# The chosen tokens' keys made token-major in four column tiles, and the shared latent copied by DMA

## The chip, the cores and the metric

One NeuronCore of a Trainium2 chip runs the whole program. The metric is the device time of one execution in microseconds (us). Five engines work side by side and meet at semaphores: TensorE (PE, matmul; PEld is its weight load), VectorE (DVE), ScalarE (ACT), GpSimd (POOL) and SyncE (SP, which here only issues DMAs).

## The reference, cut to what matters

The reference is a two-layer network on `x` of shape (8, 512, 128): a WKV layer and a quantised linear layer, then an attention layer of three branches and a recurrent layer. The change touches the attention layer alone. Of that, for one batch element:

```python
nq  = _rms(x @ w_cq, g_qnorm)                     # 512 x 96
q   = concat([nope(nq @ w_dq_nope), rope(nq @ w_dq_rope)])   # 16 heads, 32 + 64
ckv = _rms(x @ w_ckv, g_kvnorm)                   # 512 x 32, the shared latent
k1  = concat([ckv @ w_dk_nope, rope(x @ w_krope) / 16])
idx = sort(top_k(x @ w_imp, 32)); sel = x[idx]    # the 32 chosen tokens
ks  = sel @ w_selk                                # 32 x 16 heads x (32 + 64)
ks  = concat([ks[..., :32], rope(ks[..., 32:])])
vs  = sel @ w_selv
kw, vw = x @ w_wink, x @ w_winv
a1 = attn(q, k1, v1, causal); a2 = attn(q, ks, vs); a3 = attn(q, kw, vw, causal)
out = gate0 * a1 + gate1 * a2 + gate2 * a3
```

All data are float32.

## The kernel before

The main loop walks over "units". A unit is one batch element `b` (8 of them), one group `g` of four heads (4 groups), one causal branch `a` (0 for `a1`, 1 for `a3`) and one set of 128-row query blocks (three sets: block 3, blocks 0 and 1, block 2): 8 x 4 x 2 x 3 = 192 units. Round `i` of the loop makes the scores of unit `i + 2` (`score`, L777), lowers them by mask and row maximum on VectorE (`lowered`, L789), exponentiates on ScalarE (`raised`, L798), scales the rows on GpSimd (`normalised`, L807), transposes the probabilities of unit `i` on TensorE (`weigh`, L821), copies them out on ScalarE (L599), and after every third unit multiplies with the values (`values`, L835). Feeds between them (`group_inputs`) make the next group's queries, keys and values: `qR` and `k3R` by `rotary` (L630), `qN`, `qA` and `k3N` by `plain` (L606, copied out at L608), the values at L661.

The order of instructions on PE, DVE, ACT and POOL is the order in which the Python code issues them (`manual_schedule`), and each engine runs its own list in that order. The rest of the work runs as generators ("chains") beside the units: `layer0` (WKV, L315 to L388, and the quantised linear layer, L399 to L425, with `mx_quantize`, L140 to L170), `before` (which is `prepare(b)`: normalisation, latents, shared keys, gate, top-k, chosen keys), and `recurrence`. Four times in a round `advance` lets each chain take one step, if the number that it yielded has been counted down. A chain that yields `M` goes on only at the fourth place of a round; one that yields 0 goes on at the next place. `need(name, b)` advances all chains until something is ready, and in it `M` steps run at once.

Of `prepare(b)` two parts concern the change.

`shared_keys(b)`, run some rounds ahead of the batch element's first scores: `k1R` is the rotated shared key (two matmuls L630, `turn` on VectorE L615 to L622 and on GpSimd L621 and L623). Then `k1N`, the shared latent in four copies below one another, 128 rows: a matmul (`k1l`, L708) of the latent, rows 96 to 127 of `nqT`, with `rep`, four 32x32 identities side by side, and a copy out on ScalarE with a scale per row (`g4`, L709). Between its three parts it yields `M`, so each has a round to itself. The scores of branch 0 read `k1N` against `qA`.

`chosen_keys(b)`: `sel` (128 features x 32 tokens, written by ScalarE at L535) is the moving operand; each of 12 matmuls has a 128x128 block of weights as its stationary operand and gives 32 columns. Eight (L680, `sk`) make the two halves of the rotary part, each half in a PSUM tile of its own, turned from PSUM on VectorE (L615, L616, L620, L622) and finished on GpSimd (L621, L623) as `sR`; four (L689, `sNp`) make the other part, copied out by ScalarE (`sN`, L690). Each of these three is followed by a yield of `M`. Then `sV` (a matmul at L694, eight VectorE instructions of 32 rows at L698). `sR` and `sN` are stationary operands of the chosen branch's scores (`chosen`, L739), which go through PSUM into 32x32 block transposes on VectorE (L745), a softmax (L748 to L756) and the product with `sV` (L722). `attend_chosen(b, 0)` calls `need("chosen", b)`.

A float32 matmul stands in the trace as two records, so 12 matmuls are 24 of PE. In shapes such as `32*128` the first number is the rows of the stationary block and the second its columns.

PSUM: the pool `ps_t` has three buffers, shared by all that `bank` hands out; the scores have four single buffers (`ps_s`), the output one (`ps_o`). The queue of SP carries the loads of `x`, and writes `x1all` and `h2all` of each batch element to DRAM for the tail, in the order of the program.

Of the kernel before, what the change touches and what calls it, by code (L numbers as in the profile page):

```python
# [11 lines left out]
FP = mybir.dt.float32  # L12
U32 = mybir.dt.uint32
AF = mybir.ActivationFunctionType
# [9 lines left out]
HG = 4  # L24
# [34 lines left out]
def adaln_kernel(ctx: ExitStack, tc: tile.TileContext, x, pa, pb, pc, pt, out):  # L59
# [10 lines left out]
    mask = const.tile([128, T], FP, name="mask")  # L70
    wmix = {n: [const.tile([128, 128], FP, name=f"{n}{i}") for i in range(2)] for n in ("wkT", "wvT", "wrT")}
    wn, u, nu = (const.tile([128, 1], FP, name=n) for n in ("wn", "u", "nu"))
    rep = const.tile([128, 128], FP, name="rep")
    wqT = const.tile([128, 128], FP, name="wqT")
    gbias = const.tile([128, B], FP, name="gbias")
    sil0 = const.tile([128, B], FP, name="sil0")
# [96 lines left out]
    with tc.tile_pool(name="start", bufs=1) as p1, tc.tile_pool(name="startps", bufs=2, space=PSUM) as pp:  # L173
        wa = p1.tile([128, _width(A_COLS)], FP, name="wa")
        wa2 = p1.tile([128, _width(A2_COLS)], FP, name="wa2")
        WA = _views(wa, A_COLS) | _views(wa2, A2_COLS)

        load(0)
        nc.sync.dma_start(out=wa, in_=pa[:, 0 : _width(A_COLS)])
        load(1)  # L180
        nc.sync.dma_start(out=wa2, in_=pa[:, _width(A_COLS) :])
        for t, p in ((wb, pb), (wt, pt), (wc, pc)):
            nc.sync.dma_start(out=t, in_=p)
        make_identity(nc, ident)


        for l in range(2):
            c_in = WA[f"cT{l}"]

            sg = p1.tile([128, B], FP, name=f"sg{l}")  # L190
            S.activation(sg, c_in, AF.Tanh, scale=0.5)
            si = sil0 if l == 0 else p1.tile([128, B], FP, name="sil1")
            V.tensor_scalar(sg, sg, 0.5, 0.5, ALU.mult, ALU.add)
            V.tensor_tensor(si, sg, c_in, ALU.mult)
            ps = pp.tile([128, 6, B], FP, name=f"modps{l}", tag="modps")
            for j in range(6):
                PE.matmul(ps[:, j, :], lhsT=WA[f"wmod{l}"][:, j * 128 : (j + 1) * 128], rhs=si, start=True, stop=True)
            m = mods[l]
            V.tensor_copy(m, ps)
            for j in (1, 4):  # L200
                V.tensor_scalar(m[:, j, :], m[:, j, :], 1.0, None, ALU.add)
            for j in (2, 5):
                sgn = p1.tile([128, B], FP, name=f"sgn{l}{j}")
                V.tensor_scalar(sgn, m[:, j, :], 0.0, 2.0, ALU.is_ge, ALU.mult)
                mag = p1.tile([128, B], FP, name=f"mag{l}{j}")
                V.scalar_tensor_tensor(mag, m[:, j, :], -1.0, m[:, j, :], ALU.mult, ALU.max)
                V.tensor_scalar(mag, mag, 0.25, None, ALU.max)
                V.scalar_tensor_tensor(m[:, j, :], sgn, -1.0, mag, ALU.add, ALU.mult)


        for n, m in (("wkT", "tmk"), ("wvT", "tmv"), ("wrT", "tmr")):
            om = p1.tile([128, 1], FP, name=f"om_{m}")
            V.tensor_scalar(om, WA[m], -1.0, 1.0, ALU.mult, ALU.add)
            V.tensor_scalar(wmix[n][0], WA[n], WA[m], None, ALU.mult)
            V.tensor_scalar(wmix[n][1], WA[n], om, None, ALU.mult)
        S.activation(wn, WA["w"], AF.Exp)
        V.tensor_scalar(wn, wn, -1.0, None, ALU.mult)
        V.tensor_copy(u, WA["u"])
        V.tensor_scalar(nu, WA["u"], -1.0, None, ALU.mult)


        wq = p1.tile([128, 4, 32], FP, name="wq")
        for _ in mx_quantize(
            wq, WA["fw"].rearrange("p (n k) -> p n k", k=32), 4,
            lambda n: p1.tile([128, 4, 32], FP, name=f"q{n}_w"), "w",
        ):
            pass
        wps = pp.tile([128, 128], FP, name="wps", tag="modps")
        PE.transpose(wps, wq.rearrange("p n k -> p (n k)"), ident)
        S.copy(wqT, wps)  # L230
        V.tensor_scalar(gbias, mod0[:, 5, :], WA["fbias"], None, ALU.mult)

        ps = pp.tile([QL, H * KVL], FP, name="foldp", tag="foldp")
        for g in range(NG):
            PE.matmul(
                ps[:, g * 128 : (g + 1) * 128], lhsT=WA["wdqT"][:, g * QL : (g + 1) * QL],
                rhs=WA["wdkT"][:, g * 128 : (g + 1) * 128], start=True, stop=True,
            )  # L240
        wd = WB["wd"]
        qscale = 1.0 / math.sqrt(HD)
        gq = p1.tile([QL, 1], FP, name="gq")
        V.tensor_scalar(gq, WB["g"][0:QL, :], qscale, None, ALU.mult)
        S.activation(wabs, ps, AF.Copy, scale=gq)
        V.tensor_scalar(wd[0:QL, :], wd[0:QL, :], gq, None, ALU.mult)
        V.tensor_scalar(wd[QL:128, 0:512], wd[QL:128, 0:512], WB["g"][QL:128, :], None, ALU.mult)
        V.tensor_scalar(WB["wkr"], WB["wkr"], 1.0 / H, None, ALU.mult)

        for j in range(HG):  # L250
            V.tensor_copy(rep[QL:128, j * KVL : (j + 1) * KVL], ident[QL:128, QL:128])

        for n in ("ufT", "uiT", "ucT", "uoT", "bf", "bi"):
            V.tensor_scalar(WC[n], WC[n], 0.5, None, ALU.mult)

        G.memset(mask, 0.0)
        G.affine_select(
            mask, mask, pattern=[[-1, T]], compare_op=ALU.is_ge, fill=NEG, base=T - 128, channel_multiplier=1
        )
# [33 lines left out]
    def bank(shape, name):  # L293
        return ps_t.tile(shape, FP, name=name, tag="t")
# [305 lines left out]
        else:  # L600
            V.tensor_copy(dst, src)

    def plain(pool, name, b, g, src, w):

        ps = bank([128, T], f"{name}p_{b}_{g}")
        PE.matmul(ps, lhsT=w[:, g * 128 : (g + 1) * 128], rhs=src, start=True, stop=True)  # L606
        dst = pool.tile([128, T], FP, name=f"{name}_{b}_{g}", tag=name)
        S.copy(dst, ps)  # L608
        return dst

    def turn(i, dst, ps, tabs, pool, tags, key):
# [13 lines left out]
    def rotary(pool, name, key, src, w, temps):  # L625

        dst = pool.tile([128, 2, T], FP, name=f"{name}_{key}", tag=name)
        for i in range(2):
            ps = bank([128, T], f"{name}m{i}_{key}")
            PE.matmul(ps, lhsT=w[:, i * 128 : (i + 1) * 128], rhs=src, start=True, stop=True)  # L630
            turn(i, (dst[:, 0, :], dst[:, 1, :]), ps, (cosT, sinT), *temps, f"{name}_{key}")
            if i == 1:
                rot_of[name] = dst
            yield

    def group_inputs(b, g):
# [5 lines left out]
        yield from rotary(pq, "qR", f"{b}_{g}", nq, wq_r[:, hs], (p1, ("rt0", "rt1")))  # L642
        qN = plain(pq, "qN", b, g, nq, wq_n)
        yield
        qA = plain(pq, "qA", b, g, nq, wabs)
        q_of[b, g] = rot_of["qR"], qN, qA
        yield
        yield from rotary(p1, "k3R", f"{b}_{g}", hT, ww_r[:, hs], (p1, ("rt0", "rt1")))
# [21 lines left out]
    def chosen_keys(b):  # L670

        _, _, gate, sel = made_of[b]
        shape = [128, NG, KEEP]
        tabs = [tab[:, 0:KEEP].unsqueeze(1).to_broadcast(shape) for tab in (cosT, sinT)]
        sR = pb_.tile([128, 2, NG, KEEP], FP, name=f"sR_{b}", tag="sR")
        for i in range(2):
            yield M
            ps = bank(shape, f"sk{i}_{b}")
            for g in range(NG):
                PE.matmul(  # L680
                    ps[:, g, :], lhsT=ws_r[:, (2 * g + i) * 128 : (2 * g + i + 1) * 128], rhs=sel[:, 0, :],
                    start=True, stop=True,
                )
            turn(i, (sR[:, 0], sR[:, 1]), ps, tabs, pw, ("p2", "p3"), f"sk_{b}")
        yield M
        sN = pb_.tile([128, NG, KEEP], FP, name=f"sN_{b}", tag="sN")
        ps = bank([128, NG, KEEP], f"sNp_{b}")
        for g in range(NG):
            PE.matmul(ps[:, g, :], lhsT=ws_n[:, g * 128 : (g + 1) * 128], rhs=sel[:, 0, :], start=True, stop=True)  # L689
        S.copy(sN, ps)  # L690
        yield M
        sV = pb_.tile([128, 2, NG, VD], FP, name=f"sV_{b}", tag="sV")
        ps = bank([128, NG, HG, VD], f"sv_{b}")
        PE.matmul(ps, lhsT=sel, rhs=WB["wselv"], start=True, stop=True)  # L694
        for h in range(2):
            for j in range(HG):
                at = home(j, h)
                V.tensor_scalar(sV[at, h], ps[at, :, j, :], gate[at, 1:2], None, ALU.mult)  # L698
        chosen_of[b] = (sR[:, 0], sR[:, 1], sN), sV

    def shared_keys(b):

        hT, nqT, _, _ = made_of[b]
        for _ in rotary(pb_, "k1R", f"{b}", hT, WB["wkr"], (pw, ("p2", "p3"))):
            yield M
        k1N = pb_.tile([128, T], FP, name=f"k1N_{b}", tag="k1N")
        ps = bank([128, T], f"k1l_{b}")
        PE.matmul(ps, lhsT=rep[QL:128, :], rhs=nqT[QL:128, :], start=True, stop=True)  # L708
        S.activation(k1N, ps, AF.Copy, scale=WB["g4"])  # L709
        k1_of[b] = rot_of["k1R"], k1N  # L710

    def home(j, h):
# [401 lines left out]
```

## Time and profile before

| | before |
|---|---|
| median of 3 runs | 1780.53 us (1780.38 to 1781.57) |
| profiled execution | 1776.72 us |
| its span | 1774.9 us |
| TensorE clock granted, mean | 0.963 |
| PE, DVE, ACT, POOL busy | 93%, 71%, 66%, 52% |
| DMA queue of SP, share of 16 engines | 2.9% |

A busy share is an average, and matmuls are pipelined, so PE at 93% is not PE at its peak. The chain of waits is followed back from the last instruction: at each step it goes to what released that instruction, or to the one before it on its engine. A microsecond taken from a piece of the chain can shorten the run; one taken from work off the chain cannot, until it is on it. The first 95 us are the start (loads, layer 0 of the first elements); the units run from there to about 1740 us.

### The profile page before, as it was taken

What the parts mean: (1) busy time and instruction counts of PE and PEld (TensorE: products, weight loads), DVE (VectorE), ACT (ScalarE), POOL (GpSimd) and SP (SyncE); (2) the same over time, 40 slices, a digit from 0 to 9 for tenths busy, and PEclk for the clock granted to TensorE, in tenths of its full rate; (3) what the DMA queues carried; (4) which work ended last, traced back from release to release, by engine and by line L of the source; (5) the groups of instructions that cost most, each with busy time, mean ns of one, the idle gap of its engine ahead of it and who ended that gap; (6) DMA issues with size and microseconds to landing.
All of it is one profiled execution on the core that took longest, in us unless ns stands there. A gap on an engine that the chain in (4) does not pass through costs nothing.

```text
span 1774.9 us, 40101 instructions
## 1 busy us (share of the span) xinstructions
PE 1651.0 (93%) x14865; PEld 964.7 (54%) x14865; DVE 1253.5 (71%) x4246; ACT 1166.3 (66%) x3262; POOL 914.6 (52%) x1370
## 2 busy tenths in 40 slices
PE   4388999899999999999999999999999999999997
PEld 2245555555555555555555555555556555655663
DVE  6678777875876698776886777776885766665542
ACT  1244777566765777667776677677666777767782
POOL 1145556544754475644755455545656455545651
PEclk8698999899999999999999999999999999999998
DMA  4000000000000000000000000000000000000012
GB/s 168 1 1 1 2 1 1 7 2 13 2 1 7 13 2 1 2 13 7 1 2 1 13 1 2 1 14 7 1 1 1 13 8 1 2 13 8 13 37 66
DMA packets 13395, 20.24 MB, mean 11 GB/s; under 512 B 784, under 2 KB 8976, under 8 KB 13072
## 3 DMA queue, kind: packets, MB, share of 16 engines
q1 hardware_dynamic: 13200, 17.67, 2.9%
q8 instruction: 119, 1.95, 0.4%
q14 instruction: 76, 0.62, 0.1%
HBM read 11.90 MB, written 5.77 MB: 10 GB/s over the span
## 4 chain that ended last, share of the span: by engine, by line
PE 71%; DVE 20%; POOL 3%; ACT 3%; issue 2%; DMA 1%; SPq 0%; POOLq 0%; ACTq 0%; DVEq 0%
PE s L777 23%; PE t L821 13%; PE o L835 7%; DVE p L789 6%; PE qRm L630 2%; PE s L739 2%; PE k3Rm L630 2%; PE v1p L661 2%; PE v0p L661 2%; PE op L846 2%; PE o L722 1%; PE qAp L606 1%; PE k3Np L606 1%; POOL p L807 1%; PE qNp L606 1%
## 5 line engine op out<-in xcount | busy, mean ns | idle before, releaser
L807 POOL TENSOR_SCALAR p<-p,rs 128x512 f32<-128x512 f32 (+3 forms) x1024 | 556.2, 564 | 503.6 <-DVE rs L803 318.6
L789 DVE CUSTOM_DVE_ANT_0 p<-s,mask 128x512 f32<-128x512 f32 (+3 forms) x1024 | 443.0, 478 | 223.4 <-PE s L777 221.5
L798 ACT ACTIVATE p<-p,nm 128x512 f32<-128x512 f32 (+3 forms) x1024 | 560.9, 553 | 15.3 <-DVE nm L789 15.3
L599 ACT COPY pT<-t 128x384 f32<-128x384 f32 (+1 forms) x768 | 355.4, 522 | 200.2 <-PE t L821 198.6
L821 PE MATMUL t<-ident,p 128*128 128x128 f32 x2560 | 361.9, 279 | 18.5 <-DVE k3R L616 5.8
L821 PEld LDWEIGHTS t<-ident,p 128*128 128x128 f32 x2560 | 273.8, 141 | 141.6 <-issue 106.0
L777 PE MATMUL s<-k3R,qR 32*128 32x512 f32 (+3 forms) x2048 | 197.7, 471 | 6.4 <-DVE nm L789 5.3
L777 PE MATMUL s<-k1R,qR 32*128 32x512 f32 (+3 forms) x2048 | 192.0, 458 | 10.0 <-DVE nm L789 7.8
L798 ACT ACTIVATION_READ_ACCUMULATOR p<-p,nm 128x1 f32 x1024 | 195.8, 191 | 0.0
L835 PE MATMUL o<-pT,v 128*32 128x512 f32 (+3 forms) x2048 | 151.1, 436 | 0.0
L777 PEld LDWEIGHTS s<-k3R,qR 32*128 32x128 f32 x2048 | 100.4, 192 | 91.5 <-DVE nm L789 31.2
L777 PEld LDWEIGHTS s<-k1R,qR 32*128 32x128 f32 x2048 | 98.6, 188 | 93.6 <-issue 34.7
L835 PEld LDWEIGHTS o<-pT,v 128*32 128x32 f32 x2048 | 60.0, 109 | 109.4 <-issue 98.4
L777 PE MATMUL s<-k1N,qA 32*128 32x512 f32 (+3 forms) x1024 | 98.3, 430 | 0.0
L777 PE MATMUL s<-k3N,qN 32*128 32x512 f32 (+3 forms) x1024 | 98.2, 437 | 0.0
L789 DVE DVE_READ_ACCUMULATOR2_ANT nm<- 128x1 f32 x1024 | 83.2, 81 | 0.0
L599 ACT COPY accT<-o 128x512 f32<-128x512 f32 x32 | 18.8, 588 | 89.4 <-PE o L835 89.4
L749 POOL TENSOR_TENSOR p<-p,m 128x512 f32<-128x512 f32 x32 | 33.6, 1049 | 83.6 <-DVE m L748 83.5
L621 POOL TENSOR_TENSOR k3R<-k3R,rt_k3R 128x512 f32<-128x512 f32 x32 | 40.8, 1273 | 66.1 <-DVE rt_k3R L620 66.1
L630 PE MATMUL qRm<-nqT,wb 96*128 96x512 f32 x128 | 68.9, 621 | 2.0 <-ACT pT L599 1.0
L777 PEld LDWEIGHTS s<-k3N,qN 32*128 32x128 f32 x1024 | 56.3, 192 | 24.6 <-issue 17.3
L777 PEld LDWEIGHTS s<-k1N,qA 32*128 32x128 f32 x1024 | 55.6, 188 | 22.7 <-issue 10.1
(314 smaller groups left out, 2492.6 us busy)
## 6 DMA issues: line engine op xcount, KB each, us to landing
wb<-pb_dram SPq DMA_DIRECT2D x1, 3475.0 KB, 14.7
x<-x_dram SPq DMA_DIRECT2D x8, 256.0 KB, 3.8
x1all<-x SPq DMA_DIRECT2D x7, 256.0 KB, 2.3
h2all<-h SPq DMA_DIRECT2D x7, 256.0 KB, 2.0
h2o<-h2all SPq DMA_DIRECT2D x7, 256.0 KB, 2.6
x_first<-x1all SPq DMA_DIRECT2D x4, 256.0 KB, 4.2
out_dram<-x_first SPq DMA_DIRECT2D x4, 256.0 KB, 2.5
out_dram<-x SPq DMA_DIRECT2D x4, 256.0 KB, 2.4
```

Of the source, the lines that this page charges most:

```text
L599: S.copy(dst, src)
L606: PE.matmul(ps, lhsT=w[:, g * 128 : (g + 1) * 128], rhs=src, start=True, stop=True)
L621: G.tensor_tensor(lo, lo, r[0], ALU.subtract)
L630: PE.matmul(ps, lhsT=w[:, i * 128 : (i + 1) * 128], rhs=src, start=True, stop=True)
L661: PE.matmul(ps[:, c, :], lhsT=hT[:, cs] if i else nqT[QL:128, cs], rhs=(WB["wwinv"] if i else wv_1)[:, g * 128 : (g + 1) * 128], start=Tru ...
L739: PE.matmul(sp[h][to, :], lhsT=k[js, g, :], rhs=q[js, h * half : (h + 1) * half], start=(i == 0), stop=(i == 2), skip_group_check=True,)
L777: PE.matmul(un.s[j][:, at : at + n], lhsT=q[js, n - 128 : n], rhs=k[js, 0:n], start=(i == 0 and at == 0), stop=(i == 2), skip_group_check= ...
L789: V.tensor_tensor_reduce(out=un.p[:, j, at : at + n], in0=un.s[j][:, at : at + n], in1=mask[:, T - n :], scale=-1.0, scalar=3.4e38, op0=AL ...
L798: S.activation(p, p, AF.Exp, bias=un.nm[:, j, i : i + 1], scale=-1.0, accum_out=un.rs[:, j, i : i + 1])
L807: G.tensor_scalar(p, p, un.rs[:, j, i : i + 1], 1.0, ALU.mult, ALU.mult)
L821: PE.transpose(tp[:, k, :], un.p[:, j, at : at + 128], ident)
L835: PE.matmul(out_ps[js, c * 128 :], lhsT=v[:, c, js], rhs=pT[:, j, at[0] : at[-1] + 1 : step, :], start=not a and c == 0, stop=False, skip_ ...
```

## The change

`chosen_keys` swaps the operands: `sel` (128x32) is the stationary operand and the weights are streamed. Heads 0 to 3 of a group go to four column tiles of 32 columns, so that four matmuls write four groups of 32 PSUM partitions: four of 256 columns for the rotary part, four of 128 for the other, all in one PSUM tile, tokens in partitions. Two VectorE transposes by 32x32 blocks (128x256 into `kT`, 128x128 into `sN`) give the layout that was there before. `turn` then reads `kT` in SBUF where it read PSUM. The copy of `sN` on ScalarE is gone. The yields change: matmuls and transposes come at once, each `turn` follows at the next place of a round, and only then comes an `M`.

`shared_keys` issues four DMAs on SP's queue that copy the latent to the four row groups of `k1N`, before the rotary part; the matmul L708, the scaled copy L709 and the constant `rep` (four VectorE copies at the start) are gone, and two of three yields of `M` with them. The scale `g4` moves to the copy of `qA`: `plain` uses `activation` with AF.Copy and a scale, which is 1.0 for `qN` and `k3N` and `g4` for `qA`.

```diff
-        for j in range(HG):
-            V.tensor_copy(rep[QL:128, j * KVL : (j + 1) * KVL], ident[QL:128, QL:128])
...
-    def plain(pool, name, b, g, src, w):
+    def plain(pool, name, b, g, src, w, scale=1.0):
...
-        S.copy(dst, ps)
+        S.activation(dst, ps, AF.Copy, scale=scale)
...
-        qA = plain(pq, "qA", b, g, nq, wabs)
+        qA = plain(pq, "qA", b, g, nq, wabs, WB["g4"])
...
+        ps = bank([128, 3 * NG, 32], f"sk_{b}")
+        heads = [(w.rearrange("k (n j d) -> k j n d", j=HG, d=32), at, n) for w, at, n in ((ws_r, 0, 2 * NG), (ws_n, 2 * NG, NG))]
+        for w, at, n in heads:
+            for j in range(HG):
+                PE.matmul(
+                    ps[32 * j : 32 * (j + 1), at : at + n, :], lhsT=sel[:, 0, :], rhs=w[:, j], start=(at == 0), stop=True,
+                    skip_group_check=True,
+                )
+        kT = work("p2", [128, NG, 2, KEEP], f"kT_{b}")
+        V.transpose(kT.rearrange("p g i k -> p (g i k)"), ps[:, 0 : 2 * NG, :].rearrange("p n d -> p (n d)"))
+        sN = pb_.tile(shape, FP, name=f"sN_{b}", tag="sN")
+        V.transpose(sN.rearrange("p g k -> p (g k)"), ps[:, 2 * NG :, :].rearrange("p n d -> p (n d)"))
         sR = pb_.tile([128, 2, NG, KEEP], FP, name=f"sR_{b}", tag="sR")
+        yield 0
         for i in range(2):
-            yield M
-            ps = bank(shape, f"sk{i}_{b}")
-            for g in range(NG):
-                PE.matmul(
-                    ps[:, g, :], lhsT=ws_r[:, (2 * g + i) * 128 : (2 * g + i + 1) * 128], rhs=sel[:, 0, :],
-                    start=True, stop=True,
-                )
-            turn(i, (sR[:, 0], sR[:, 1]), ps, tabs, pw, ("p2", "p3"), f"sk_{b}")
-        yield M
-        sN = pb_.tile([128, NG, KEEP], FP, name=f"sN_{b}", tag="sN")
-        ps = bank([128, NG, KEEP], f"sNp_{b}")
-        for g in range(NG):
-            PE.matmul(ps[:, g, :], lhsT=ws_n[:, g * 128 : (g + 1) * 128], rhs=sel[:, 0, :], start=True, stop=True)
-        S.copy(sN, ps)
-        yield M
+            turn(i, (sR[:, 0], sR[:, 1]), kT[:, :, i, :], tabs, pw, ("p3", "p3") if i == 0 else ("p3", "p1"), f"sk_{b}")
+            yield 0 if i == 0 else M
...
     def shared_keys(b):
-        for _ in rotary(pb_, "k1R", f"{b}", hT, WB["wkr"], (pw, ("p2", "p3"))):
-            yield M
         k1N = pb_.tile([128, T], FP, name=f"k1N_{b}", tag="k1N")
-        ps = bank([128, T], f"k1l_{b}")
-        PE.matmul(ps, lhsT=rep[QL:128, :], rhs=nqT[QL:128, :], start=True, stop=True)
-        S.activation(k1N, ps, AF.Copy, scale=WB["g4"])
+        for j in range(HG):
+            nc.sync.dma_start(out=k1N[j * KVL : (j + 1) * KVL, :], in_=nqT[QL:128, :])
+        for i, _ in enumerate(rotary(pb_, "k1R", f"{b}", hT, WB["wkr"], (pw, ("p2", "p3")))):
+            if i == 0:
+                yield M
```

More of the change, by code (lines that the diff above doesn't have):

```diff
@@ L72, in adaln_kernel @@
     wn, u, nu = (const.tile([128, 1], FP, name=n) for n in ("wn", "u", "nu"))
-    rep = const.tile([128, 128], FP, name="rep")
     wqT = const.tile([128, 128], FP, name="wqT")
```

## The prediction, made before the changed kernel ran

> **What bounds the kernel now.** I read the page first, the chain of waits above all.
>
> ```profile
> PE 1651.0 (93%) x14865; PEld 964.7 (54%) x14865; DVE 1253.5 (71%) x4246; ACT 1166.3 (66%) x3262; POOL 914.6 (52%) x1370
> ...
> PE 71%; DVE 20%; POOL 3%; ACT 3%; issue 2%; DMA 1%; SPq 0%; POOLq 0%; ACTq 0%; DVEq 0%
> ```
>
> The chain is PE for seven tenths and DVE for two. Summed in eight stretches from 95 to 1720 us, PE has about 1190 of 1625 us, or 73%. So PE work taken away in the middle of the run is worth about 0.73 of itself, and ACT work (3%) next to nothing. Next I asked the chain, in order of time, for the pieces that the change removes. Around the start of batch element 4 (counted from 0) they stand in it one after the other:
>
> ```profile
> 936.77 0.85 PE sk L680 x8
> ...
> 944.59 0.85 PE sk L680 x8
> 945.44 1.80 PE k3Rm L630 x4
> 947.24 0.56 PE o L722 x8
> ...
> 952.53 0.81 PE sNp L689 x8
> 953.35 0.94 PE k3Np L606 x2
> ```
>
> The columns are start, length, what. The three groups of 8 records cost 2.51 us of chain here, and PE waits for nothing between 928 and 962 us. The same groups stand in the chain at elements 5, 6 and 7, two of the three at element 3; `k1l` stands there at 285.79, 473.59, 666.36, 865.10, 1074.54, 1285.42 and 1482.08 us, 1.05 us each time. The first three elements look different. For element 0 the chain has
>
> ```profile
> 144.27 3.62 PE sk L680 x16
> 147.90 1.72 PE sNp L689 x8
> 149.62 0.02 issue
> 149.64 0.28 ACT sN L690
> 149.92 0.04 issue
> 149.96 2.07 PE sv L694 x2
> 152.03 2.56 PE s L739 x48
> ```
>
> that is PE at half clock (the windows from 144 to 152 us show 0.50 granted), and for element 1
>
> ```profile
> 348.40 1.66 POOL q L160
> 350.06 0.07 issue
> 350.13 1.60 POOL q L164
> 351.73 0.02 issue
> 351.75 0.69 DVE q L168
> 352.45 0.20 DVE sR L615
> ```
>
> Here the chosen keys' turn stands on DVE behind the quantiser's `q`, which waits for POOL; PE is idle 4.29 us until `sR` is there (354.23). Element 2 repeats it (3.72 us idle, until 542.42).
>
> **The change, part by part.** The changed program's order of instructions, laid beside the old one, gives positions and no times.
>
> *The chosen keys on PE.* Removed: 24 records, 2.5 us at full clock (0.85 + 0.85 + 0.81). Added: 16 records in four column tiles. No row has this shape (128 rows, 32 columns, 256 or 128 streamed). The nearest is `o` L722: 8 records of 256 columns in four tiles, 0.56 us. I take 0.56 for the rotary part and half, 0.28, for the other: 0.84. From below: `o` L835, 32 records of 512+384+256+128 columns in four tiles, 2.29 us in the chain, by columns 384/1280 x 2.29 = 0.69. From above: tiles that do not overlap, each load (L835's mean 109 ns) behind the other, 16 x 0.109 = 1.74. Gain 1.67 per element (0.8 to 1.8); for elements 3 to 7: 8.4 us.
>
> L722's 0.56 lies above what its columns need: `op` L846 takes 3.45 us for 8 records of 512, so 0.43 each, and two records of 256 in a row are 0.43; 0.13 us is for getting in and out. The Trainium skill (TensorEngine Tiling (Array Packing), Key Properties) says that changing the tiling mode drains TensorE, which speaks against the change, since the old groups had the 128x128 shape of their neighbours; if each group paid two drains of 0.13 beyond the row, the sum would be 8 x 0.26 = 2.1 us less. The same page's Performance Considerations advise just this swap for 32 streamed columns.
>
> *Element 0.* 16 records at half clock 1.7 us, so done at 145.95; two transposes on DVE 0.65, three short steps (`rsqrt`, 0.16 to 0.20 each) 0.6, turn 0.4, three more 0.6, turn 0.4: 148.6; POOL two of 0.46, the first starting the chosen scores: about 149.2 against 152.03. Gain 2.8.
>
> *Elements 1 and 2.* In the new order the transposes and turns stand before the quantiser's first `q` on DVE, and POOL's work for `sR` between its two long ones. Element 1: `z` ends at 344.35, transposes 0.65, rotary 1.2, `e` 1.04, turn 0.4, `m` 1.78: 349.4; POOL's first `q` 1.66, `sR` 0.47: PE goes on at 351.6 against 354.23. Element 2: 535.26 + 0.65 + 0.44 + 0.4 + 0.78 = 537.5, + 1.65 + 0.47 and issue = 539.8 against 542.42. Gain 2.6 each. But the `q` steps passed over are only put behind the chosen scores, where DVE has still to do them, ahead of row maxima that PE waits for. I take half of these and of element 0: (2.8 + 5.2) x 0.5 = 4.0, bounds 0 and 8; the clock that the wait pulls down (`s` L739 2.81 us at 354 against 1.46 at 956) could give 2 x 1.35 more.
>
> *The shared latent.* Removed from PE: 1.05 us at elements 1 to 7, 7.35; nothing at element 0, where the first scores wait for POOL's `k1R` (96.52 to 99.01), which is no earlier. Added: four DMAs of 64 KB. The row of `h2all` (256 KB) lands in 2.0 us, that of `x1all` in 2.3, and one issue holds SP 0.34 us, so some 3.7 us from `nqT` to the last copy (4 x 0.34 + 2.3). Element 0: `nqT` ends at 88.21, copies by 91.9, first read at 100.0. Element 1: the latent is made ahead of 285.7 and read at 305.57; the later ones have more (element 2 from 473.5 to 517.0, element 4 from 865.0 to 940.7). So it is covered everywhere, by 8 us at element 0; uncovered it would cost at most 3.7 each. On SP the four stand before or behind DRAM copies that have been issued by then, as the tile order shows; what is behind them (`x1all`, a load five elements' buffers ahead) is not waited for until much later.
>
> *VectorE.* Added per element: a transpose of 128x256, row L745, 0.43, and one of 128x128, from L745 and L759 (0.70 for 512) about 0.29; starts lie closer, so 0.65. Four turns of 0.28 now read SBUF instead of PSUM; rows of 512 columns say 0.69 for either, but 1.64 where POOL runs beside (L166): so 0 to 1.6 more. Elements 3 to 7 at DVE's 20% of the chain: 5 x 0.65 x 0.2 = 0.65 us, at worst 5 x 2.25 = 11. `rep` (4 x 0.17 at 15 us) lies under the loads. What stands behind a transpose that waits for `sk` is `lowered`; DVE has waited 221.5 us for those scores over the run, so it has room on the mean.
>
> *ScalarE.* `qA` goes from a copy (590 ns) to a scale per row (`k1N`'s 696): 32 x 0.106 = 3.4. `qN`, `k3N` get a constant scale: L327, constant scale from PSUM, 593 against 586: 0.4; bounded by the scaled row, 6.4. Gone: `k1N` 5.6, `sN` 2.1. Net -3.9 (to +2.1) on 3% of the chain: nothing.
>
> *Order.* Chosen and shared keys need one to three rounds less, and all chains shift by up to a round against the units. The tail is the same instruction for instruction. I count nothing for it; ACT and DVE pieces fall elsewhere, some us either way.
>
> **Sum.** (8.4 + 7.35) x 0.73 = 11.5, plus 4.0, less 0.65: 14.9 us. The profiled span 1774.9 becomes 1760.0, its execution 1776.7 becomes 1761.8. The median shown lies 3.8 above that execution, so 1765.6; I say 1765.5.
>
> **Rivals.**
> - *Half the gain.* The tiles run one after the other (1.74 instead of 0.84, 4.5 us less at the five elements), or the shift of the chains costs some us. With (3.85 + 7.35) x 0.73 = 8.2 and nothing of the 4.0: 1780.5 - 8.2 + 0.65 = 1773. For it: no row has the shape. Against: L835 and L722 show four tiles overlapped.
> - *Nothing.* PE's pieces go, but the next wait ends where they ended: 1780.5 within 3.6. For it: 27% of the chain is not PE. Against: the stretch at 928 to 962 is PE without a gap.
> - *Slower: VectorE takes the bound at the element changes.* In the new order `sV` (eight, 2.88 us from first start to end) stands before the four 512-wide row maxima of the new element's first unit, where it stood after the next unit's, and the transposes stand before the old element's last. If DVE is then last, elements 3 to 7 pay 2.88 + 0.65 each, 17.7, gain nothing from the chosen keys and the latent, and only 4.0 + 2 x 1.05 x 0.73 = 5.5 is kept: 1780.5 + 12.2 = 1793. It decides from 1.9 us of DVE lag per element (14.9 / 8). For it: DVE is 20% of the chain, 80% busy from 300 to 400 us. Against: it waits for PE 3.46 us just before `sV` at 952.
>
> **Chances.** Forecast (gain 7.5 to 27, 1753.5 to 1773) 0.62; half gain 0.15; nothing 0.10; slower 0.13. About 0.2%, 3.6 us, can be told from no change. So faster 0.77, same 0.10, slower 0.13. The forecast's own range is 1754 to 1773. The range given holds also half the gain and the edge of nothing: 1753 to 1780; below it lies full value with the clock kept, 1780.5 - 15.75 - 8 - 2.7 = 1754, and above it most of slower.
>
> **What would show it.** `sk` as 16 records in the shape 128*32, 0.7 to 0.9 us at full clock; `k1l` gone and no wait of PE for a DMA; PE's wait for `sR` at elements 1 and 2 down from 4.29 and 3.72 to about 2; DVE's share of the chain not above 22%. Wrong: `sk` over 1.5 us, or a longer wait of PE for `nm` (the row maxima) at the changes.

## The result and the profile after

| | before | after |
|---|---|---|
| median (range, 4 runs each) | 1780.45 us (1779.3 to 1781.57) | 1768.53 us (1765.78 to 1771.47) |
| ratio, 95% interval | | 0.9941 [0.9929, 0.9954] |
| profiled execution, its span | 1776.72, 1774.9 us | 1771.47, 1769.7 us |

The changed kernel is faster by 10.5 us (8.2 to 12.6 by the interval). This gain is taken from the ratio, as are the gains given beside ratios below; the ratio is an estimate of its own and not the quotient of the two medians, which lie 11.9 us apart. Two kernels of one series are compared by their medians. The profiled execution is the slowest of its four. When the same kernel was run again, it came to 0.9967 [0.9955, 0.9979], 5.9 us; the two intervals do not overlap. So a ratio can differ by 0.0026, or 4.6 us, between two series of runs of one kernel. The experiments ran in three series of four kernels, each on one chip. Kernels are compared below first with those of their own series, and each ratio is against the kernel before on that chip. The line numbers of after are 3 or 4 lower: L777 is now L774, L739 L736, L835 L832, L821 L818, L789 L786, L807 L804, L524 L520, and `turn` is L611 to L619.

One slip in the text on the change, and in two expectations below: `shared_keys` had two yields of `M`, and one of them is gone, not two of three. That one yield turns out to matter.

From the page of after, its span, the busy time of each engine and the chain by engine:

```profile
span 1769.7 us, 39998 instructions
...
PE 1626.1 (92%) x14785; PEld 941.1 (53%) x14785; DVE 1254.3 (71%) x4258; ACT 1165.9 (66%) x3246; POOL 919.0 (52%) x1370
...
PE 68%; DVE 22%; POOL 3%; ACT 3%; issue 2%; DMA 1%; SPq 0%; POOLq 0%; ACTq 0%; DVEq 0%
```

PE is busy 24.9 us less (1651.0 to 1626.1), and VectorE is busy for the same time as before to 0.8 us. But the chain did not simply get shorter by PE's part. Summed over stretches from 95 to some 1712 us, PE's pieces fell from 1188.8 to 1145.4 us, and VectorE's rose from 327.2 to 365.5, GpSimd's from 43.8 to 48.3. The two stretches are equally long, so what PE's pieces lose the others gain: 43 us. That is twice what the change took out of the chain: `sk`, `sNp` and `k1l` had 24.6 us there before, and the new `sk` has 3.2.

The parts of the change, from the views of the tiles `sk`, `sR` and `k1N` (after; duration in ns as min/median/max, first and last start, shapes):

```profile
L676 PE MATMUL sk<-wb,sel x128: 272/382/636, 146.6 to 1532.4; 128*32 128x256 f32 x64, 128*32 128x128 f32 x64
L681 DVE STREAM_TRANSPOSE kT<-sk x8: 437/440/451, 148.2 to 1533.4; 128x256 f32<-128x256 f32 x8
L683 DVE STREAM_TRANSPOSE sN<-sk x8: 267/271/276, 148.6 to 1533.8; 128x128 f32<-128x128 f32 x8
```

```profile
L611 DVE TENSOR_TENSOR sR<-kT,wt x8: 273/283/1364, 149.2 to 1535.2; 128x128 f32<-128x128 f32 x8
```

```profile
L703 SPq DMA_DIRECT2D k1N<-nqT x32: 507/588/1349, 89.8 to 1466.0; - x32
...
DMA to landing us min/median/max: 1.9/2.0/3.3
```

The 16 records of an element overlap in their four tiles: in the chain at element 3 and at element 7 they are one piece of 0.80 us. The transposes take 0.44 and 0.27 us. The four copies land in 2.0 us, and no wait of PE for a DMA appears. The line to note is the turn, L611: six take 0.27 to 0.28 us, those of elements 1 and 4 take 1.35 and 1.36.

The chain of after at element 0 (start, length, what):

```profile
146.61 1.55 PE sk L676 x16
...
150.42 0.46 POOL sR L617
...
150.93 2.91 PE s L736 x48
```

From the first `sk` to the chosen scores it is 4.32 us, where it was 7.76 (144.27 to 152.03). This is the stretch that the prediction worked out, and it comes 3.4 us shorter. But `sk` itself starts 2.34 us later, so the scores start 1.1 us earlier.

PE's waits, in total, times and longest, first before, then after:

```profile
PE s L777 <- DVE nm L789: 13.0, 17, 1.9
...
PE s L739 <- POOL sR L621: 8.0, 2, 4.3
```

```profile
PE s L736 <- POOL sR L617: 16.1, 3, 8.6
...
PE s L774 <- DVE nm L786: 10.5, 16, 1.5
...
PE s L736 <- DVE slT L520: 6.6, 2, 4.3
```

The wait for the row maxima `nm` did not grow. The wait for `sR`, which was to halve, doubled. And a new reader waits for `slT` (L520), a copy of 128x4 that belongs to the top-k of the next element and frees a buffer of `ps_t`: the chosen scores. Before, PE waited for `slT` 6.8 us in all, at other matmuls and never more than 2.5 at once; after it is 10.1, and 4.3 at once.

Element 1 is one of the places of the wait for `sR`. The chain of after there:

```profile
344.83 0.85 DVE z L146
...
346.24 0.58 DVE rt_qR L616
...
348.45 1.27 DVE sR L611
349.73 0.20 DVE sR L612
...
350.68 1.44 POOL q L159
352.12 0.87 POOL sR L617
...
353.04 1.06 PE s L736 x9
```

The order is as the prediction had it: turn, `q`, `sR` on GpSimd, scores. The sum was to end at 351.6, and ended at 353.04 against 354.23 before. The turn was taken at 0.4, and its first two pieces alone took 1.47 (1.27 + 0.20); GpSimd's `sR` was taken at 0.47 and took 0.87. The quantiser's `z` ended 1.33 us later than the sum took it to (345.68 for 344.35), and `m` and `q` were 1.3 us shorter than taken. At element 2 the scores start at 541.63 against 542.42. There the pieces from `z` to the scores were as long as taken (4.4 us for 4.5), but `z` ended at 537.26, 2.0 us later than in the sum. Earlier by 1.19 and 0.79 us, then, in place of 2.6 each. PE waits longer all the same, since it comes to the two places 3.7 and 5.6 us sooner than before.

The prediction's strongest stretch was element 4, where PE stood in the chain without a gap from 928 to 962 us. The chain of after, same stretch:

```profile
930.09 0.36 DVE kT L681
...
932.88 1.29 DVE sR L611
...
936.08 1.26 POOL q L159
...
938.21 4.09 POOL p L804 x8
942.30 1.25 POOL q L163
...
947.55 2.23 PE s L774 x28
```

PE is out of the chain from 918 to 947 us. The new transpose, the turn (stretched again, 1.29 us) and the quantiser's two long `q` on GpSimd stand there, with the scaling of a unit's rows, `p`, between the two. That did not undo the gain: from the first values matmul of element 3 to that of element 4, which holds this stretch, after gained 3.5 us, as the table shows.

What several kernels make of this can be read from their profiles (one execution each) at one mark: the first values matmul (`o`, L835 before) of each batch element. Its time before, and how much later (+) or earlier (-) it is in the others, in us:

| element | before | after | all old yields | yield back at 1, 2 | yield back elsewhere | slot by ScalarE |
|---|---|---|---|---|---|---|
| 1 | 360.15 | -1.6 | +1.8 | -1.4 | -0.4 | -3.8 |
| 2 | 573.66 | -1.9 | +1.9 | -2.3 | -0.8 | -4.3 |
| 3 | 779.16 | +1.4 | +1.9 | -2.5 | +2.6 | -1.3 |
| 4 | 987.76 | -2.1 | -2.1 | -2.5 | -0.5 | -4.8 |
| 5 | 1197.24 | -0.7 | -6.0 | -5.2 | -0.4 | -8.3 |
| 6 | 1406.30 | -0.0 | -9.9 | -9.8 | -3.6 | -15.7 |
| 7 | 1592.99 | -5.0 | -12.5 | -14.8 | -6.8 | -20.7 |

A second profiled execution of after lies up to 2.3 us from its column, and the execution of "slot by ScalarE" is the fastest of its five, 3.5 us below their median. After gains and gives back: 3.3 us on the way to element 3, 1.4 to element 5, 0.7 to element 6. With all yields in their old places nothing is gained up to element 3, and then 4.0, 3.9, 3.9 and 2.6 us per element. The other columns are explained below.

### The profile page after: what moved, and what is told of

Its sections match the earlier page's. It is cut to its first block, busy times and chain, and to the rows that moved or that the text cites. A ratio compares the mean times of both kernels' runs of the same rounds, so it can differ in the third digit from the quotient of the medians.

```text
span 1769.7 us, 39998 instructions
## 1 busy us (share of the span) xinstructions
PE 1626.1 (92%) x14785; PEld 941.1 (53%) x14785; DVE 1254.3 (71%) x4258; ACT 1165.9 (66%) x3246; POOL 919.0 (52%) x1370
## 4 chain that ended last, share of the span: by engine, by line
PE 68%; DVE 22%; POOL 3%; ACT 3%; issue 2%; DMA 1%; SPq 0%; POOLq 0%; ACTq 0%; DVEq 0%
PE s L774 23%; PE t L818 12%; PE o L832 7%; DVE p L786 7%; PE s L736 2%; PE qRm L626 2%; PE v1p L657 2%; PE v0p L657 2%; PE k3Rm L626 2%; PE op L843 2%; POOL p L804 1%; PE qAp L602 1%; PE o L719 1%; PE k3Np L602 1%; PE qNp L602 1%
## 5 line engine op out<-in xcount | busy, mean ns | idle before, releaser
L804 POOL TENSOR_SCALAR p<-p,rs 128x512 f32<-128x512 f32 (+3 forms) x1024 | 561.2, 568 | 497.3 <-DVE rs L800 336.8
L786 DVE CUSTOM_DVE_ANT_0 p<-s,mask 128x512 f32<-128x512 f32 (+3 forms) x1024 | 443.1, 479 | 228.7 <-PE s L774 226.9
L818 PE MATMUL t<-ident,p 128*128 128x128 f32 x2560 | 363.8, 280 | 25.2 <-DVE rt_k3R L618 5.5
L818 PEld LDWEIGHTS t<-ident,p 128*128 128x128 f32 x2560 | 274.5, 141 | 150.7 <-issue 106.6
L774 PE MATMUL s<-k1R,qR 32*128 32x512 f32 (+3 forms) x2048 | 195.4, 458 | 8.1 <-DVE nm L786 4.7
L774 PE MATMUL s<-k3R,qR 32*128 32x512 f32 (+3 forms) x2048 | 192.9, 460 | 7.2 <-DVE nm L786 5.8
L832 PE MATMUL o<-pT,v 128*32 128x512 f32 (+3 forms) x2048 | 152.8, 439 | 0.0
L774 PEld LDWEIGHTS s<-k1R,qR 32*128 32x128 f32 x2048 | 98.7, 187 | 93.3 <-issue 35.7
L774 PEld LDWEIGHTS s<-k3R,qR 32*128 32x128 f32 x2048 | 99.4, 189 | 90.5 <-DVE nm L786 35.0
L832 PEld LDWEIGHTS o<-pT,v 128*32 128x32 f32 x2048 | 60.3, 110 | 110.9 <-issue 100.0
L774 PE MATMUL s<-k1N,qA 32*128 32x512 f32 (+3 forms) x1024 | 102.1, 437 | 0.0
L774 PE MATMUL s<-k3N,qN 32*128 32x512 f32 (+3 forms) x1024 | 98.5, 434 | 0.0
L786 DVE DVE_READ_ACCUMULATOR2_ANT nm<- 128x1 f32 x1024 | 83.9, 82 | 0.0
L736 PE MATMUL s<-qR,sR 32*32 32x256 f32 x1024 | 48.8, 417 | 24.8 <-POOL sR L617 16.1
L774 PEld LDWEIGHTS s<-k1N,qA 32*128 32x128 f32 x1024 | 56.6, 189 | 24.9 <-issue 12.9
L774 PEld LDWEIGHTS s<-k3N,qN 32*128 32x128 f32 x1024 | 56.6, 190 | 22.5 <-issue 15.5
```

Of the source, the lines that this page charges most:

```text
L736: PE.matmul(sp[h][to, :], lhsT=k[js, g, :], rhs=q[js, h * half : (h + 1) * half], start=(i == 0), stop=(i == 2), skip_group_check=True,)
L774: PE.matmul(un.s[j][:, at : at + n], lhsT=q[js, n - 128 : n], rhs=k[js, 0:n], start=(i == 0 and at == 0), stop=(i == 2), skip_group_check= ...
L786: V.tensor_tensor_reduce(out=un.p[:, j, at : at + n], in0=un.s[j][:, at : at + n], in1=mask[:, T - n :], scale=-1.0, scalar=3.4e38, op0=AL ...
L804: G.tensor_scalar(p, p, un.rs[:, j, i : i + 1], 1.0, ALU.mult, ALU.mult)
L818: PE.transpose(tp[:, k, :], un.p[:, j, at : at + 128], ident)
L832: PE.matmul(out_ps[js, c * 128 :], lhsT=v[:, c, js], rhs=pT[:, j, at[0] : at[-1] + 1 : step, :], start=not a and c == 0, stop=False, skip_ ...
```

## The experiments

The first four kernels ask how much is the instructions and how much is their places. The times in their expectations start from 1780.5 us; in their series the kernel before had 1776.44, so they are to be compared as gains.

**All old yields.** After's instructions, with the yields of both parts where they were: one ahead of the chosen matmuls, one after each turn, one ahead of `sV`, two in `shared_keys`.

```diff
+        yield M
...
-        yield 0
...
-            yield 0 if i == 0 else M
+            yield M
+        yield M
...
-        for i, _ in enumerate(rotary(pb_, "k1R", ...)):
-            if i == 0:
-                yield M
+        for _ in rotary(pb_, "k1R", ...):
+            yield M
```

> The changed instructions in the old order: all yields of the chosen and the shared keys are as before, so that every other instruction keeps its place (the changed kernel moved some 550 of VectorE's). Theory 'work': the time comes from TensorE's work taken away, wherever the chains stand, so this is the changed kernel's time again, 1766 to 1771. Theory 'order costs': the work is worth more than the 12 us measured, and the shift of the chains against the units gave some of it back, so this is 1757 to 1764. Theory 'order gains': fewer rounds and the early turn at elements 1 and 2 are the gain, so this is 1774 to 1781.

1763.44 us, 0.9929 [0.9916, 0.9943]: 12.6 us faster. The work alone, without the new places, is worth as much as or more than the change as a whole. The two terms of the prediction that speak of work alone came to 11.5. As a gain this is what theory 'work' expected; the bare time lies in the range of 'order costs' only because before ran 4 us faster here.

**New places alone.** Before's instructions, with yields as after has them (both turns come right behind their matmuls; the rotary part of `shared_keys` moves behind `k1N`).

```diff
-            yield M
...
-        yield M
...
+        yield 0
+        yield 0
...
-        for _ in rotary(pb_, "k1R", ...):
-            yield M
...
+        for i, _ in enumerate(rotary(pb_, "k1R", ...)):
+            if i == 0:
+                yield M
```

> The old instructions (12 matmuls, the latent's matmul, the copies) at the new yields: the other half of the cross with the kernel before. Theory 'work': no change, 1778 to 1783. Theory 'order costs': slower than before, 1784 to 1793. Theory 'order gains': 1768 to 1775.

1780.2 us, 1.0023 [1.0013, 1.0032]: 4.1 us slower. The places by themselves cost. Work and places nearly multiply: 0.9929 x 1.0023 = 0.9952, between the two values of after.

**The latent alone.** Before with the four copies and the scale moved to `qA`; yields old.

```diff
-        PE.matmul(ps, lhsT=rep[QL:128, :], rhs=nqT[QL:128, :], start=True, stop=True)
-        S.activation(k1N, ps, AF.Copy, scale=WB["g4"])
+        for j in range(HG):
+            nc.sync.dma_start(out=k1N[j * KVL : (j + 1) * KVL, :], in_=nqT[QL:128, :])
```

> The kernel before with the latent's four DMAs alone, g4 on the copy of qA, and the three yields of the shared keys kept: TensorE loses 1.05 us at seven elements, nothing else moves. Theory 'work' by the prediction's sum: 7.35 x 0.73 = 5.4 us less, 1775. Theory 'order costs': more than its share, up to the full 7.35, 1773 to 1775. Theory 'order gains' (this has no new order): 1778 to 1782. If a DMA landed late, TensorE would wait for it and the time would be above 1781.

1771.61 us, 0.998 [0.9971, 0.9989]: 3.6 us (2.0 to 5.2). The prediction's term for it, 7.35 x 0.73 = 5.4, is above the interval by a little.

**The tiles alone.** Before with after's `chosen_keys`, its yields among it.

> The kernel before with the new chosen keys alone (column tiles, transposes, their new yields), the shared keys as they were. By the prediction's sum: 8.4 x 0.73 + 4.0 - 0.65 = 9.5 us less, 1771. Theory 'order costs': the large shift of the chains comes from the shared keys' yield, which is kept here, so 1764 to 1769. Theory 'order gains': 1773 to 1778.

1769.86 us, 0.9962 [0.995, 0.9975]: 6.7 us (4.4 to 8.9). The prediction's terms for it make 8.4 x 0.73 + 4.0 - 0.65 = 9.5. The sum of the two parts is 10.3 us; with the chosen keys' yields old as well it is 12.6, on the same chip. So their new places, the early turn among them, which was to bring 4.0, show no gain, though 2.3 us is within the noise of such a sum.

The next four kernels take the two parts' yields one by one, with after again beside them.

**After again.**

> The changed kernel itself, to stand beside the next two on one chip. Its ratio on record, 0.9941 (0.9929 to 0.9954), is the expectation of every theory. If work and order add, the earlier runs give it too: 0.9929 (old places) times 1.0023 (new places) is 0.9952.

1770.82 us, 0.9967 [0.9955, 0.9979].

**The shared keys' yield back.** After, with one line's condition gone.

```diff
-        for i, _ in enumerate(rotary(pb_, "k1R", ...)):
-            if i == 0:
-                yield M
+        for _ in rotary(pb_, "k1R", ...):
+            yield M
```

> The changed kernel with the three yields of the shared keys put back; the chosen keys at their new yields. That shift of the shared keys moves some 1000 lines of VectorE's order, the chosen keys' some 130. If the shared keys' lost rounds are what costs: 0.992 to 0.9935 of before, like the old places (0.9929). If the chosen keys' yields cost: 0.994 to 0.996. The sum of latent alone and tiles alone gives 0.998 x 0.9962 = 0.9942.

1763.38 us, 0.9928 [0.9915, 0.9942]: 7.4 us faster than after beside it. One yield, which moves no work from one engine to another, is worth that. Beside the 0.9929 of all old yields, which ran on another chip, the chosen keys' own places show no worth either way.

**The chosen keys' yields back** (as in the first diff), the shared keys' yield left out as in after.

> The other way round: the chosen keys' yields put back, the shared keys at the new ones. If the shared keys' lost rounds cost: 0.994 to 0.996 of before. If the chosen keys' yields cost: 0.992 to 0.9935.

1773.14 us, 0.9981 [0.9973, 0.999]. Slower than after beside it by 2.3 us, with intervals that overlap, and slower than either theory expected. It is the lost shared yield that costs, with either set of the chosen keys' places.

Why so much hangs on it is seen in the order of the lists. `need` and the counted rounds shift everything behind `prepare`: a comparison of VectorE's lists has some 1000 changed lines for this yield, and some 130 for the chosen keys' yields. One place where the two chains part, at the change to element 5, from the chain of after:

```profile
1186.31 0.45 PE rp L132 x4
...
1186.78 0.69 DVE x L134
...
1187.93 0.78 DVE st_p L107 x4
...
1189.82 1.03 DVE xn L119 x4
...
1192.28 4.37 PE s L774 x20
```

and with the yield back:

```profile
1182.69 0.44 PE rp L132 x4
1183.13 0.74 PE t L817 x6
...
1183.91 0.66 PE tp L127 x4
...
1186.62 3.32 PE s L773 x24
```

After has two normalisations (`x`, `xn` and the statistics `st_p`) and row maxima in one heap on VectorE, and PE's scores come behind it, 6.0 us after `rp`. With the yield back the chain stays on PE, through transposes to the scores, 3.9 us after `rp`.

**The transposes twice.** The first experiment's kernel with both transposes done a second time into a tile that nothing reads.

```diff
+        again = pw.tile([128, 3 * NG * KEEP], FP, name=f"again_{b}", tag="again")
+        V.transpose(again[:, 0 : 2 * NG * KEEP], ps[:, 0 : 2 * NG, :].rearrange("p n d -> p (n d)"))
+        V.transpose(again[:, 2 * NG * KEEP :], ps[:, 2 * NG :, :].rearrange("p n d -> p (n d)"))
```

> The kernel at the old places (ratio 0.9929) with both 32x32 block transposes done a second time into a tile that nobody reads: 0.65 us more of VectorE at each of eight elements. The prediction's price (20% of the chain): 1.0 us more, 0.9935. If VectorE ends last at the element changes, the full 5.2 us, 0.9958. The chain of the kernel at the old places has the transposes at elements 0 to 3 and TensorE's sk at 4 to 7, so I expect 0.65 x 3 to 4 = 2 to 2.6 us, 0.994 to 0.9944.

1765.34 us, 0.9937 [0.9925, 0.9949], beside 0.9929 without: 1.4 us, but the two intervals overlap and come from two chips; with both, anything from nothing to 4.6 us fits. A second set is 8 x 0.71 = 5.7 us of VectorE. A price of a quarter of it, near VectorE's 20 to 22% of the chain, agrees with this and is not shown by it; the full price (0.9958) lies outside the interval.

The last four kernels ask what the place costs by. Two of them take the yield apart by elements; two test the new wait for `slT`.

**The slot by ScalarE.** After, with the copy that frees the buffer moved off the crowded engine.

```diff
-        V.tensor_copy(slT, slps)
+        S.copy(slT, slps)
```

> The changed kernel with one copy moved from VectorE to ScalarE: slT, which frees the PSUM buffer of the top-k slots. In the changed kernel's profile TensorE waits 6.6 us before the chosen scores (twice) and 2.7 us before a k3R for this copy, which stands behind VectorE's pile. If the held buffer is what the lost round costs: 5 to 9 us less than the changed kernel, 0.992 to 0.994 of before. If the pile on VectorE itself is the cost and the buffer only the place where it shows: at most 2 us less, 0.9955 to 0.9967.

1759.55 us, 0.9892 [0.9878, 0.9906]: the lowest of all, and 8.7 or 13.3 us under after, by the one or the other of after's ratios. That is more than the expectation gave to the held buffer (0.992 to 0.994). The chain of after at the place of the longest wait for `slT`, then the chain of this kernel at the same units:

```profile
1321.51 1.21 DVE rt_f L96
...
1325.70 2.11 DVE hf L119 x4
1327.82 0.08 DVE slT L520
...
1327.94 2.78 PE s L736 x40
1330.72 3.39 PE s L774 x24
```

```profile
1310.65 0.61 DVE rt_k3R L618
...
1311.91 0.34 PE slps L518 x4
...
1314.17 1.09 PE s L736 x37
1315.27 3.23 PE s L774 x24
```

In after the copy of 0.08 us stands behind a heap of VectorE work, and the chosen scores behind the copy. Moved, it holds nobody up: no wait of the scores for `slT` is left. From the values matmul before this place to the one behind it (`o`, 1302.91 to 1334.05 us in after) after takes 31.1 us, this kernel 25.0, and the kernel before took 24.8. By the mark at element 6 it stands 15.6 us ahead of after.

**The yield back at elements 1 and 2 only.**

```diff
-            if i == 0:
+            if i == 0 or b in (1, 2):
```

> The changed kernel with the shared keys' lost yield put back at elements 1 and 2 alone. There the yield decides whether layer 0 of all later elements runs one round earlier (some 1000 lines of VectorE's order change). If that standing lag of layer 0 is the cost: like the old places of the shared keys, 0.992 to 0.994 of before. If each element's own round is the cost: near the changed kernel, 0.9955 to 0.9967.

1760.91 us, 0.9901 [0.9887, 0.9914], below what the standing lag was expected to give. In this kernel the chosen scores still wait for `slT` twice, 4.5 us in all.

**The yield back at all others** (`b not in (1, 2)`).

> The counterpart: the yield put back at elements 0 and 3 to 7, not at 1 and 2 (302 lines of VectorE's order change). Standing lag: like the changed kernel, 0.9955 to 0.9967 of before. Each element's own round: five or six of seven shares of the gain, 0.993 to 0.994.

1771.78 us, 0.9964 [0.9951, 0.9977]. The two differ by 10.9 us on one chip. The whole loss is that of the yields at elements 1 and 2; to leave it out at the others costs nothing. (0.9901 against 0.9928 would be a gain, but two series of one kernel have differed as much.) When those two are missing, layer 0's work for the elements from 2 on lies a round later, and keeps that lag to the end: in PE's order, the quantised linear layer's matmul `of` of element 2 comes after the scores of 32 units in place of 31, that of element 7 after 145 in place of 144. This fits the table: the columns part at element 3, and again from 5 on.

The traces show a part of the price. From the mark of element 2 to that of element 3, every kernel here that lacks the two yields falls back against before, by 3.1 to 6.6 us: after, in both of its executions, "new places alone", "the chosen keys' yields back", "the yield back at all others" and "the slot by ScalarE". The other seven fall back by 0.6 us at most. Between the last values matmul before element 5's mark and that mark it is the same, 1.9 to 3.9 us against 0.0. No score waits for `slT` in either stretch. The chain of the kernel with the yield back at all others at the first of the two places:

```profile
646.95 1.31 DVE ev L342
648.26 1.54 DVE cq L461
649.80 0.80 DVE gwfT L583
...
655.75 2.33 PE o L832 x32
```

and of the one with the yield back at 1 and 2 alone, up to the same values matmul:

```profile
648.55 1.50 PE s L736 x40
650.05 2.15 PE s L774 x24
652.20 2.29 PE o L832 x32
```

With the lag, layer 0's `ev`, the latents' `cq` and a gate of the recurrence, `gwfT`, stand one behind the other on VectorE ahead of PE's scores. Without it the chain stays on PE.

**Both edits**: the shared keys' yield back at all elements, and the slot by ScalarE.

> The best version by the earlier runs: the shared keys' yield back at every element (0.9928), and slT by ScalarE. That kernel's profile has 2.5 and 3.4 us of TensorE's waits for slT. If they are worth their length, 0.989 to 0.991; if VectorE's pile is behind them, 0.992 to 0.993.

1764.75 us, 0.9924 [0.9912, 0.9937], against 0.9928 for the yield alone. So the copy on ScalarE shows no worth where the order does not hold up the chosen scores: with the yield back they do not wait for `slT` at all. PE's other waits for it, 7.0 us in all, as before, are gone with the copy moved, and nothing is gained by that.

The pair shows one thing more. "The slot by ScalarE" differs from this kernel by the lost yield alone and ran on the same chip, and it is 5.2 us faster, with intervals that do not overlap. With `slT` on VectorE the lost yield costs 7.4 us; with `slT` on ScalarE it gains 5.2. So the lag is no loss in itself: it costs at the two places above and gains at others. But the wait for `slT` is not the whole cost of the order either. In the kernel with the yield back elsewhere, the chosen scores do not wait for `slT` either, and it is as slow as after; in the one with the yield back at 1 and 2 they do, and it is fast.

## Why the prediction was right, and where it was not

The forecast was 14.9 us; the runs gave 10.5, and 5.9 when repeated. Sign and the mechanism of the main term were right, two other terms were not. With nothing for the early turn the sum is 10.9, which is near 10.5 in part by luck: the work brought somewhat more, and the places, put at nothing, took some of it back. The rival "half the gain" had named this, "the shift of the chains costs some us", and 7.5 us for it; the two measured gains lie on both sides of that.

- *The work taken from PE, (8.4 + 7.35) x 0.73 = 11.5.* Right in the sum. `sk` was put at 0.84 us and takes 0.80, and the work in the old places brings 12.6. The worth of 0.73 per microsecond held in the sum, not place by place: with the old places the first elements gain nothing, and the later ones 2.6 to 4.0 where (1.67 + 1.05) x 0.73 makes 2.0. Why it is spread so was not tested, so that the sum agrees is no proof of the price. The parts alone gave less than their terms, 3.6 for 5.4 and 6.7 for 9.5, of which 6.1 were PE's work and 4.0 the early turn.
- *The tiles overlap.* Right. The Trainium skill (TensorEngine Tiling (Array Packing), Key Properties) says that a change of the tiling mode drains TensorE. The prediction would have added two drains of 0.13 us to each group, which makes 0.84 + 0.26 = 1.10 us. The trace has 0.80, so no run here shows a drain beyond what the forecast's row already held.
- *The copies are covered.* Right, at every element, with 2.0 us to landing. One issue held the queue 0.59 us where 0.34 was taken; at element 0 the last copy landed 7.8 us ahead of the first read, for 8 in the text.
- *The early turn, 4.0.* Not borne out. Three pairs differ by the chosen keys' places alone: 0.9928 against 0.9929, after against "the chosen keys' yields back", and the sum of the two parts against all old yields. They give 0.2, 2.3 and -2.3 us, none clear of noise and none as much as 4.0. The working took the place where the stretch begins from the old trace; `z` ended 1.3 us later at element 1 and 2.0 at element 2. At element 1 the turn and GpSimd's `sR` were also under-sized by 1.5 us, since their times were read from rows in which nothing ran beside them; the range for the turns ("0 to 1.6 more") was in the text, and the lower end was taken.
- *"Order … I count nothing for it."* This step failed. It holds for the chosen keys' places. For the one yield of the shared keys it is wrong by 7.4 us on one chip, and by 10.9 between the elements where it is missing, as long as `slT` is copied by VectorE. The text saw that the chains shift by up to a round against the units, and called it "some us either way"; it is a lag that stays, with a price at some places and a gain at others.
- *VectorE's work, 0.65.* Not contradicted. A second set of transposes cost 1.4 us for eight elements, within a noise of some 3.
- *The rival "slower"* had VectorE last at the element changes. Its mechanism is there, at places that it did not name: heaps of VectorE work at one change and inside element 5 (1186 and 1313 to 1328 us) and GpSimd and VectorE in the place of PE at element 4. It was priced for `sV` and the transposes at each of elements 3 to 7; `sV` stands in the chain of after once, at 743 us, for 2.8 us (in the second execution twice, for 5.2). To stand in the chain is no price by itself: the chosen keys' `kT`, `sN`, `sR` and `sV` make 15.0 us of the chain in after and 14.8 in the fastest kernel.
- *What would show it.* Four signs came as told: `sk` 0.80, no matmul for the latent and no wait for a DMA, VectorE at 22%, no longer wait for `nm`. One came the other way, the wait for `sR` at elements 1 and 2.

How the lag turns into time is only partly settled. The wait for `slT` is one way, since its removal alone brings the changed kernel to the lowest time, but its length does not tell the cost: 4.5 us of it stand in a fast kernel, and none in a slow one. The heap on VectorE between elements 2 and 3 is seen in every trace with the lag and was not tested by an edit. Where the lag gains, once `slT` is out of the way, is open. The best two, the slot by ScalarE (0.9892) and the yield back at elements 1 and 2 (0.9901), were not tried together.

## What to carry to other kernels

Where an order is written out by hand, test a change of work and a change of places apart: here the work gave 12.6 us, and one lost yield cost 7.4 in one comparison and 10.9 in another, and gained 5.2 once a copy of 128x4 had moved to another engine. PE's share of the chain gave the price of work taken from PE to about a third (3.6 for 5.4, 6.7 for 6.1, 12.6 for 11.5), where the shared keys' yields stayed in their places. If a tiny copy frees a PSUM buffer that others share, put it on the engine whose list is clear at that place, and look for it in the waits by the reader's name, since the copy itself is short and looks harmless; but try it, for here it was worth 8.7 us or more in one order and nothing in another.

## What was not expected of the hardware

A VectorE instruction with both inputs in SBUF can stand still beside GpSimd. VectorE and GpSimd in the timeline of after at element 1 (start, length, line, operation):

```profile
346.75 0.67 DVE L618 TENSOR_TENSOR rt_qR<-qRm,wt 128x512 f32<-128x512 f32 x1
...
348.38 1.35 DVE L611 TENSOR_TENSOR sR<-kT,wt 128x128 f32<-128x128 f32 x1
349.65 0.28 DVE L612 TENSOR_TENSOR sR<-kT,wt 128x128 f32<-128x128 f32 x1
```

```profile
346.90 1.27 POOL L617 TENSOR_TENSOR qR<-qR,rt_qR 128x512 f32<-128x512 f32 x1 [1.75 <-DVE rt_qR L616]
348.13 1.44 POOL L619 TENSOR_TENSOR qR<-qR,rt_qR 128x512 f32<-128x512 f32 x1
```

`rt_qR` reads PSUM (`qRm`) and keeps its 0.67 us beside GpSimd. The turn reads SBUF (`kT`), starts 0.25 us after GpSimd's `qR` and ends 0.16 us after it (349.73 against 349.57): it waits for the whole instruction. The same operation takes 0.28 us when GpSimd is done. Before the change the turn read PSUM, and a step of it that began while GpSimd was at work took its 0.28 us (`rt_sk` from 1158.58 to 1158.86, beside a GpSimd instruction from 1158.35 to 1158.94). So it is the change, which moved the turn's input to SBUF, that opened it to this. The Trainium skill (SBUF — State Buffer, Who interferes with whom) says that a VectorE instruction with two SBUF inputs contends with a GpSimd instruction that reads SBUF, that the ports they share are an exclusive lock, and that the order of issue decides who blocks. The trace agrees, with 1.35 against 0.28 us.

A wait of PE can be paid again behind it by the granted clock: in after at element 1 that is 0.53 in the window from 350 to 353 us, where PE idles, and 0.50 from 353 to 357. The 48 records of the chosen scores then take 2.81 us of the chain, where they took 1.46 before at element 4 (955.90).
